# One scan through both states in twelve steps of a chunk, and wider GpSimd operands, in a bidirectional Mamba kernel

## The chip, the cores and the metric

The kernel runs on one core of a Trainium2 chip. Its time is the device time of one execution in microseconds. The engines of the core work side by side, each through its own queue in order, and wait for one another by semaphores: TensorE (PE, with its weight loads as PEld), VectorE (DVE), ScalarE (ACT), GpSimd (POOL) and SyncE (SP), which here only issues DMAs.

## The reference

The input x has 2 batches of 2048 tokens of 256 channels. A block with adaptive layer norm mixes the tokens by a Mamba layer in both directions and then runs a mixture of experts. The part that matters here is the recurrence, once forwards (weights `f_`) and once over the reversed tokens (`b_`):

```python
xz = x @ W_in.T;  xp, z = split(xz)                     # 512 inner channels
xc = silu(depthwise_conv4(xp) + b_conv)
dt, Bm, Cm = split(xc @ W_x.T, [16, 32])                # 16 states
dt = softplus(dt @ W_dt.T + b_dt);  A = -exp(A_log)
def step(h, inp):                                       # h: batch, channel, state
    dt_t, u_t, B_t, C_t = inp
    h = h * exp(dt_t[:, :, None] * A) + (dt_t * u_t)[:, :, None] * B_t[:, None, :]
    return h, einsum('bdn,bn->bd', h, C_t)
y = (ys + xc * D) * silu(z)
out = y @ W_out.T
```

So for every channel and each of 16 states there is a recurrence h[t] = decay[t] * h[t-1] + input[t] along 2048 tokens, in two batches and two directions. After it come `x + 0.5 * (forward + backward)`, a second layer norm, the gated experts (2 of 8 for a token) and a shared expert.

## The kernel before

The scan part is one hand-ordered program. Tokens are cut into chunks of 512: two directions, two batches and four chunks of tokens make 16 chunks, numbered in the order in which they are done. A chunk is 32 **steps**. Channels lie on the 128 partitions in four blocks d; states are taken two at a time (NG = 2, eight groups g). A step is one block and one group, and steps run over pairs of blocks (p), then groups, then the two blocks of the pair: an even step has the first block of a pair, the odd step after it the second, with the same two states.

What a step s does, by function:

- `inputs` (L412): GpSimd makes `db` = du times B for both states, 128x1024, three steps ahead. B is one row of numbers per state, spread over the partitions by a DMA (`load_b`), one tile for the two steps of a pair. `db` has ten buffers.
- `decays` (L429): ScalarE makes exp(dt * A), one ACTIVATE (L435) per state, 128x512, into a PSUM bank. Even and odd steps have two banks each (`banks`, L285), one tile per state.
- `scans` (L438): VectorE runs one scan (L449) per state, each from the state `hl` that the chunk before left.
- `weigh_own` (L451) or `weigh` (L457): the result times C, on VectorE per state (L455) or on GpSimd for both (L460), back into `db`. `on_pool` says which: at most odd steps it is GpSimd, at most even ones VectorE.
- `carry` (L462): ScalarE keeps the last column as the state for the next chunk (L466, L470).
- `sums` (L474): PE transposes `db` and adds all states up in PSUM (L482); this frees the `db` buffer.

After chunk 0, the four steps of two groups (one for each pair, steps 6, 7, 18 and 19) are **turned**: their operand comes from ScalarE and PE (`operands`), and the decays go into `db` in its place.

Everything else is woven into the loop over steps (L769) at written places. Three of these matter. At steps 20, 22, 24 and 26 a part of the next chunk's softplus is made: `softplus_in` (L289) takes the bank pair that the following odd step would have, ScalarE writes a sum and a logarithm into its two banks (L292, L293), and `softplus_out` (L295) works on them in three VectorE instructions (L298, L299, L300) after the scans of that step. At step 12 ScalarE runs a Silu over the next chunk's convolution (L242), with a table load on either side; at step 14 PE projects it (`dbc`, L253) and ScalarE copies the result out (L258) a step or two later. Evictions of PE's other banks by ScalarE stand behind the decays of each step.

In one turn of the loop the order is: DMAs of B and C, GpSimd's weighing of step s-2, its inputs of step s+3, the state of step s-1 (ScalarE), softplus inputs, the scans of s, softplus outputs, VectorE's weighing of s, the decays of s+1, evictions, the sums of s-4, and other units.

Of the kernel before, what the change touches and what calls it, by code (L numbers as in the profile page):

```python
# [8 lines left out]
F32 = mybir.dt.float32  # L9
AF = mybir.ActivationFunctionType  # L10
# [5 lines left out]
P = 128  # L16
# [7 lines left out]
TC = 512  # L24
# [16 lines left out]
def kernel(  # L41
# [28 lines left out]
    nc.vector.memset(eps, EPS)  # L70
    one = const.tile([P, 1], F32, tag="one", name="one")
    nc.vector.memset(one, 1.0)

    def bc(ap, n):

# [2 lines left out]
    def tiled(ap):  # L78

        return ap.rearrange("(j p) c -> p j c", p=P)  # L80

# [14 lines left out]
    with tc.tile_pool(name="mw", bufs=1) as mw, tc.tile_pool(name="mw2", bufs=2) as mw2, \  # L98
# [185 lines left out]

        def banks(s, name):  # L285

            return [ps_a.tile([P, TC], F32, tag=f"da{s % 2}_{n}", name=f"{name}_{n}") for n in range(NG)]

        def softplus_in(i, d, s):  # L289
            v = ready[i]  # L290
            v["sl"] = banks(s, f"sl{i}_{d}")
            nc.scalar.activation(v["sl"][0], v["e"][:, d, :], AF.Identity, bias=one)  # L292
            nc.scalar.activation(v["sl"][1], v["e"][:, d, :], AF.Ln, bias=one)  # L293

# [115 lines left out]
            live["C", n] = v  # L410

        def inputs(s):  # L412
            i, _, g, d = steps[s]
            db = m2.tile([P, NG, TC], F32, tag="db", bufs=NDB, name=f"db{s}")
            if not turned_step(s):
                nc.gpsimd.tensor_tensor(db, bc(ready[i]["du"][:, d, :], NG), live["B", s // 2], ALU.mult)  # L416
            live["db", s] = db

        def operands(s):

            if turned_step(s):
                i, _, _, d = steps[s]
                live["op", s] = banks(s, f"op{s}")
                for n, op in enumerate(live["op", s]):
                    for j in range(JC):
                        transpose(op[:, j * P:(j + 1) * P],
                                  ready[i]["ab"][:, n, j, d % 2 * P:(d % 2 + 1) * P], ident)

        def decays(s):  # L429
            i, _, g, d = steps[s]  # L430
            w = weights[chunks[i][0]]
            da = [live["db", s][:, n, :] for n in range(NG)] if turned_step(s) else banks(s, f"da{s}")
            for n in range(NG):
                m = g * NG + n
                nc.scalar.activation(da[n], ready[i]["dt"][:, d, :], AF.Exp, scale=w["a"][:, d, m:m + 1])  # L435
            live["da", s] = da

        def scans(s):  # L438
            i, _, g, d = steps[s]
            hl, da = state[chunks[i][:2]][0], live.pop(("da", s))  # L440
            x = live.pop(("op", s)) if turned_step(s) else [live["db", s][:, n, :] for n in range(NG)]
            h = x if turned_step(s) else da
            if on_pool(s):
                live["h", s] = m2.tile([P, NG, TC], F32, tag="h", bufs=3, name=f"h{s}")
                h = [live["h", s][:, n, :] for n in range(NG)]
            live["hs", s] = h
            for n in range(NG):
                m = g * NG + n
                nc.vector.tensor_tensor_scan(h[n], da[n], x[n], hl[:, d, m:m + 1], ALU.mult, ALU.add)  # L449

        def weigh_own(s):  # L451
            _, _, g, d = steps[s]
            if not on_pool(s):
                for n, h in enumerate(live["hs", s]):
                    nc.vector.tensor_tensor(live["db", s][:, n, :], h, live["C", s // 2][:, n, :], ALU.mult)  # L455

        def weigh(s):  # L457
            _, _, g, d = steps[s]
            if on_pool(s):
                nc.gpsimd.tensor_tensor(live["db", s], live.pop(("h", s)), live["C", s // 2], ALU.mult)  # L460

        def carry(s):  # L462
            i, _, g, d = steps[s]
# [130 lines left out]
                                     scale=v["y"][:, j, :], bias=v["mr"][:, j, :])  # L594

        def load_x(b, q):
            xt = m2.tile([P, JC, C], F32, tag="db", bufs=NDB, name=f"xt{b}_{q}")
            nc.sync.dma_start(out=xt, in_=tiled(x[b, q * TC:(q + 1) * TC, :]))
            return xt

        def norms(b, q, xt, xn):

# [13 lines left out]
            rsqrt_start(v)  # L616
            yield
            rsqrt_end(v)
            if xn is None:
                xn = m2.tile([P, JC, C], F32, tag="db", bufs=NDB, name=f"xo{u}")  # L620
            normalize(xn, v, xt)
            nc.sync.dma_start(out=tiled(xn_d[b][q]), in_=xn)

# [14 lines left out]
        make_rates(0)  # L638
        for n in range(4 * ND):
            make_conv(0, n)  # L640
        front = norms(0, 0, xts[0, 0], xns[0])
        next(front)
        next(front)
        for q in range(1, 3):
# [36 lines left out]
        def others():  # L681

            todo = [(0, 1), (0, 2), (0, 3), (1, 0), (1, 1)]
            live = []
            while todo or live:
                while todo and len(live) < 2:
                    k = todo.pop(0)
                    live.append(norms(*k, xts.pop(k), None))
                    if len(todo) > 1:
                        xts[todo[1]] = load_x(*todo[1])  # L690
                for g in list(live):
                    if next(g, 0) == 0:
                        live.remove(g)
                    yield
# [40 lines left out]
        for d in range(2):  # L735
            softplus_in(0, d, 1)
            softplus_out(0, d)
            input_(0, d)
        for s in range(3):
            inputs(s)  # L740
        decays(0)
        settle(False)
# [26 lines left out]
        for s in range(NST + 4 + SPC):  # L769
# [5 lines left out]
                weigh(s - 2)  # L775
            if s % 2 == 0 and s // 2 + 2 < NST // 2:
                load_c(s // 2 + 2)
            if s + 3 < NST:
                inputs(s + 3)
            smooth = (i + 1, soft[k]) if k in soft and i + 1 < NCH else None  # L780
            if i == 0 and k in first_soft:
# [547 lines left out]
```

## Time and profile before

| what | value |
|---|---|
| median of 3 runs | 2474.25 us (2471.53 to 2476.05) |
| the profiled execution: time, span | 2474.34 us, 2472.6 us |
| busy over the span: VectorE, GpSimd, PE, ScalarE | 2030.8, 1885.0, 1986.4, 1625.5 us |
| L416, operand on GpSimd, 128x1024 | 452 of 2361 ns |
| L449, scans, 128x512 | 1024 of about 1270 ns |
| L435, decays, 128x512 | 1024, 688 to 717 ns |
| L460, weighing on GpSimd | 252 of 2362 ns |

A group's row names the line, the engine, the operation, what it writes and reads, how often; then busy microseconds, mean nanoseconds of one, and the idle time of the engine just before such instructions, with what ended most of it. An instruction in order of time is shown by its start and its duration in microseconds, with the idle time before it and its releaser in brackets. A busy share says how full an engine is, not that it sets the pace.

### The profile page before, as it was taken

How to read it: one execution, taken by the hardware profiler on the slowest of the kernel's cores; microseconds unless marked ns; L12 is line 12 of the kernel's file. 1: busy time of each engine (PE TensorE's matmuls, PEld its weight loads, DVE VectorE, ACT ScalarE, POOL GpSimd, SP SyncE). 2: the span in 40 equal slices, each digit the busy share in tenths (PEclk: the TensorE clock that was granted, in tenths of full speed). 3: DMA queues.
4: the chain of work that ended last, by engine and by line, in shares of the span. 5: the costliest groups of instructions: out<-in, count | busy, mean ns of one | idle time of the engine just before them, and what ended most of it. 6: DMA issues, size and time to landing. Idle time of an engine off the chain costs nothing. (4 is left out here: it accounts for less than half of the span.)

```text
span 2472.6 us, 30346 instructions
## 1 busy us (share of the span) xinstructions
PE 1986.4 (80%) x9512; PEld 1372.8 (56%) x9512; DVE 2030.8 (82%) x2679; ACT 1625.5 (66%) x3377; POOL 1885.0 (76%) x991
## 2 busy tenths in 40 slices
PE   5457878788887879788887978888765487999999
PEld 2134545565555556555554656555555255788885
DVE  5499998989999999999999999999996776322333
ACT  5557787777778787777878777787753235353331
POOL 0367998989999999999999999999996405331304
PEclk9677899888998889899988989899877688999999
DMA  4344448485444454545444444444443501687863
GB/s 164 125 149 146 145 163 252 160 252 164 155 154 164 146 186 166 170 156 170 154 153 163 164 164 152 166 158 146 166 150 101 171 1 64 203 263 237 269 185 102
DMA packets 239974, 403.08 MB, mean 163 GB/s; under 512 B 38818, under 2 KB 171938, under 8 KB 239812
## 3 DMA queue, kind: packets, MB, share of 16 engines
q1 hardware_dynamic: 220724, 370.72, 46.0%
q0 software_dynamic: 6144, 16.79, 2.0%
q10 hardware_dynamic: 12944, 13.64, 1.6%
q8 instruction: 75, 1.23, 0.2%
q14 instruction: 87, 0.71, 0.1%
HBM read 346.54 MB, written 54.53 MB: 162 GB/s over the span
## 5 line engine op out<-in xcount | busy, mean ns | idle before, releaser
L416 POOL TENSOR_TENSOR db<-du,B 128x1024 f32<-128x1024 f32 x452 | 1060.0, 2361 | 13.6 <-DMA B<-bcs 13.6
L460 POOL TENSOR_TENSOR db<-h,C 128x1024 f32<-128x1024 f32 x252 | 595.1, 2362 | 66.9 <-issue 53.8
L435 ACT ACTIVATE da<-dt,w_a 128x512 f32<-128x512 f32 x904 | 594.8, 688 | 77.7 <-DVE dt L300 46.0
L482 PE MATMUL y<-ident,db 128*128 128x128 f32 x4096 | 567.7, 287 | 38.5 <-POOL db L460 36.0
L482 PEld LDWEIGHTS y<-ident,db 128*128 128x128 f32 x4096 | 504.8, 150 | 158.9 <-issue 100.8
L449 DVE TENSOR_TENSOR_SCAN da<-da,hl,db 128x512 f32<-128x512 f32 x460 | 563.9, 1273 | 4.9 <-POOL db L416 3.7
L449 DVE TENSOR_TENSOR_SCAN h<-da,hl,db 128x512 f32<-128x512 f32 x444 | 540.7, 1268 | 16.2 <-ACT da L435 16.2
L455 DVE TENSOR_TENSOR db<-da,C 128x512 f32<-128x512 f32 x460 | 293.1, 680 | 17.7 <-DMA C<-bcs 10.9
L236 PE MATMUL psc<-xp,w_conv 128*128 128x512 f32 x512 | 235.4, 603 | 10.3 <-ACT xp L225 6.4
L219 PE MATMUL psx<-xT,w_in 128*128 128x512 f32 x256 | 155.5, 727 | 100.3 <-ACT hl L470 86.9
L1041 POOL DMA_INDIRECT xs<-xs,slot x64 | 62.2, 972 | 197.3 <-DVE own L1028 95.1
L354 PE MATMUL psz<-w_in,xT 128*128 128x512 f32 x256 | 151.8, 726 | 54.0 <-ACT bT L317 32.7
L1166 POOL DMA_INDIRECT two<-ys,slot x64 | 63.0, 984 | 162.9 <-DVE hs L1068 65.5
L306 POOL TENSOR_TENSOR du<-dt,xc 128x512 f32<-128x512 f32 x64 | 81.1, 1267 | 98.3 <-DVE dt L300 97.7
L236 PEld LDWEIGHTS psc<-xp,w_conv 128*128 128x128 f32 x512 | 94.0, 193 | 108.1 <-issue 96.1
L253 PE MATMUL psd<-xc,w_x 128*48 128x512 f32 x128 | 95.8, 919 | 67.4 <-ACT hl L470 47.5
L382 PE MATMUL pso<-w_out,yg 128*128 128x256 f32 x512 | 118.4, 385 | 23.3 <-ACT e L276 23.1
L219 PEld LDWEIGHTS psx<-xT,w_in 128*128 128x128 f32 x256 | 49.8, 223 | 154.8 <-ACT hl L470 109.2
L1117 DVE COPY gT<-qgT 128x512 f32<-128x512 f32 x46 | 31.8, 692 | 121.3 <-PE qgT L846 121.1
L1062 PE MATMUL pg<-fxT,s 128*128 128x512 f32 x256 | 122.9, 638 | 0.0
L1142 ACT ACTIVATE hT<-qh,bs 128x256 f32<-128x256 f32 x92 | 38.6, 471 | 122.6 <-PE qh L1103 119.7
L382 PEld LDWEIGHTS pso<-w_out,yg 128*128 128x128 f32 x512 | 95.6, 192 | 38.5 <-ACT e L276 26.1
(200 smaller groups left out, 3221.5 us busy)
## 6 DMA issues: line engine op xcount, KB each, us to landing
C<-bcs SPq DMA_DIRECT2D x256, 512.0 KB, 4.3
B<-bcs SPq DMA_DIRECT2D x226, 512.0 KB, 4.4
we<-in_w_dram SPq DMA_DIRECT2D x138, 256.0 KB, 3.7
acc<-acc SPq DMA_DIRECT2D x32, 512.0 KB, 5.2
xs<-ident SPq DMA_DIRECT2D x2, 5888.0 KB, 23.7
xg<-xs SPq DMA_DIRECT2D x46, 256.0 KB, 3.8
ys<-yo ACTq DMA_DIRECT2D x46, 256.0 KB, 3.0
xn<-xn SPq DMA_DIRECT2D x16, 512.0 KB, 5.6
```

The lines of the kernel that those rows point to most:

```text
L219: nc.tensor.matmul(ps, w["in"][:, k, d * P:(d + 1) * P], v["xT"][:, k, :], start=(k == 0), stop=(k == KC - 1))
L236: nc.tensor.matmul(ps, w["conv"][:, d, k, :], v["xp"][:, d, k:k + TC], start=(k == 0), stop=(k == 3))
L253: nc.tensor.matmul(ps[:RK + 2 * NS, :], w["x"][:, d, :], v["xc"][:, d, :], start=(d == 0), stop=(d == ND - 1))
L354: nc.tensor.matmul(ps, v["xT"][:, k, j * P:(j + 1) * P], w["in"][:, k, DI:2 * DI], start=(k == 0), stop=(k == KC - 1))
L382: nc.tensor.matmul(ps[:, n, :], v["yg"][:, d, n * P:(n + 1) * P], wo[:, d, :], start=(d == 0), stop=(d == ND - 1))
L416: nc.gpsimd.tensor_tensor(db, bc(ready[i]["du"][:, d, :], NG), live["B", s // 2], ALU.mult)
L435: nc.scalar.activation(da[n], ready[i]["dt"][:, d, :], AF.Exp, scale=w["a"][:, d, m:m + 1])
L449: nc.vector.tensor_tensor_scan(h[n], da[n], x[n], hl[:, d, m:m + 1], ALU.mult, ALU.add)
L455: nc.vector.tensor_tensor(live["db", s][:, n, :], h, live["C", s // 2][:, n, :], ALU.mult)
L460: nc.gpsimd.tensor_tensor(live["db", s], live.pop(("h", s)), live["C", s // 2], ALU.mult)
L482: nc.tensor.matmul(ys["y"][j // 2][:, j % 2, d % 2 * P:(d % 2 + 1) * P], src[:, j * P:(j + 1) * P], ident, is_transpose=True, start=(first ...
L1062: nc.tensor.matmul(ps, s12[:, n, k, m * P:(m + 1) * P], xTs[b, q][:, k, :], start=(k == 0), stop=(k == KC - 1))
```

## The change

At an odd step that GpSimd weighs and that is not turned (twelve in each chunk), both states are scanned by one instruction of 1024 elements. So that the second state doesn't go on from the end of the first, ScalarE sets up the seam: it puts decay * state into the first input of the second state and writes zero for its first decay. The odd steps' two banks become one tile. GpSimd makes the operands of an even step and the odd step after it in one instruction, into a tile for both (five buffers of twice the size); the norms ahead of the scans use such tiles for their input and output.

```diff
         def banks(s, name):
-            return [ps_a.tile([P, TC], F32, tag=f"da{s % 2}_{n}", name=f"{name}_{n}") for n in range(NG)]
+            if s % 2:
+                v = ps_a.tile([P, NG, TC], F32, tag="da1", name=name)
+                return [v[:, n, :] for n in range(NG)], v.rearrange("p n t -> p (n t)")
+            return [ps_a.tile([P, TC], F32, tag=f"da0_{n}", name=f"{name}_{n}") for n in range(NG)], None
+
+        def through(s):
+            return s % 2 == 1 and on_pool(s) and not turned_step(s)
...
         def inputs(s):
-            db = m2.tile([P, NG, TC], F32, tag="db", bufs=NDB, name=f"db{s}")
+            db = m2.tile([P, 2, NG, TC], F32, tag="db", bufs=NDB // 2, name=f"db{s}")
             if not turned_step(s):
-                nc.gpsimd.tensor_tensor(db, bc(ready[i]["du"][:, d, :], NG), live["B", s // 2], ALU.mult)
-            live["db", s] = db
+                nc.gpsimd.tensor_tensor(
+                    db, ready[i]["du"][:, d:d + 2, :].unsqueeze(2).to_broadcast([P, 2, NG, TC]),
+                    live["B", s // 2].unsqueeze(1).to_broadcast([P, 2, NG, TC]), ALU.mult)
+            for e in range(2):
+                live["db", s + e] = db[:, e, :, :]
...
         def decays(s):
-            for n in range(NG):
+            for n in reversed(range(NG)) if through(s) else range(NG):
                 m = g * NG + n
                 nc.scalar.activation(da[n], ready[i]["dt"][:, d, :], AF.Exp, scale=w["a"][:, d, m:m + 1])
-            live["da", s] = da
+            if through(s):
+                m = g * NG + 1
+                nc.scalar.activation(db[:, 1, 0:1], da[1][:, 0:1], AF.Identity,
+                                     scale=hl[:, d, m:m + 1], bias=db[:, 1, 0:1])
+                nc.scalar.copy(da[1][:, 0:1], zero)
+            live["da", s] = da, both
...
         def scans(s):
+            if through(s):
+                nc.vector.tensor_tensor_scan(v.rearrange(flat), both, db.rearrange(flat),
+                                             hl[:, d, m:m + 1], ALU.mult, ALU.add)
+                return
...
         def load_x(b, q):
-            xt = m2.tile([P, JC, C], F32, tag="db", bufs=NDB, name=f"xt{b}_{q}")
+            xt = m2.tile([P, 2, JC, C], F32, tag="db", bufs=NDB // 2, name=f"xt{b}_{q}")
...
-        for s in range(3):
+        for s in (0, 2):
             inputs(s)
...
-            if s + 3 < NST:
+            if s % 2 == 1 and s + 3 < NST:
                 inputs(s + 3)
```

## The prediction

> **What bounds the kernel now.** I read the slices of the page first, then one steady stretch of busy times, the groups, and single instructions in order of time. The chain that ended last covers only the mixture of experts at the end, so it says nothing of the scans.
>
> ```profile
> span 2472.6 us, 30346 instructions
> ...
> DVE  5499998989999999999999999999996776322333
> ACT  5557787777778787777878777787753235353331
> POOL 0367998989999999999999999999996405331304
> ...
> L449 DVE TENSOR_TENSOR_SCAN da<-da,hl,db 128x512 f32<-128x512 f32 x460 | 563.9, 1273 | 4.9 <-POOL db L416 3.7
> L449 DVE TENSOR_TENSOR_SCAN h<-da,hl,db 128x512 f32<-128x512 f32 x444 | 540.7, 1268 | 16.2 <-ACT da L435 16.2
> ```
>
> VectorE and GpSimd are both full from slice 3 to slice 30 (about 120 to 1900 us), ScalarE is not. The stretch from 800 to 1200 us gives the shares:
>
> ```profile
> core 0: us, PE busy (x) PEld busy (x) DVE busy (x) ACT busy (x) POOL busy (x), PEclk, DMA share, GB/s
> 800.00:1200.00 400.00, 335.24 (x1690) 222.04 (x1689) 389.14 (x418) 318.15 (x671) 391.66 (x176) 0.90 0.49 164
> ```
>
> VectorE 97%, GpSimd 98%, ScalarE 80%. Which of the two full engines sets the pace is told by who waits: the scans wait 3.7 us for GpSimd's operands in the whole run, and 16.2 us for ScalarE's decays. GpSimd works three steps ahead. So VectorE sets the pace, and what moves the end is time taken from VectorE's queue or a new wait put into it.
>
> **One scan in place of two.** Twelve odd steps in each of 16 chunks, 192 in all. Start to start, the two scans of such a step take 1.190 and 1.175 us. What one element costs is read from two scans of other lengths:
>
> ```profile
> L996 DVE TENSOR_TENSOR_SCAN upto<-going,both x2: 424/424/424, 2039.4 to 2106.5; 128x128 f32<-128x128 f32 x2
> L1012 DVE TENSOR_TENSOR_SCAN end<-ones,nt x2: 174/174/174, 2044.8 to 2112.2; 128x8 f32<-128x8 f32 x2
> ```
>
> (424 - 174) / 120 = 2.083 ns an element; 512 more elements on 1.175 us make 2.242 us. A pair of 2.365 us becomes 2.242: 0.123 us saved, at most 23.7 us in 192 steps.
>
> **GpSimd's operands for two channel blocks at once.** 226 instructions of 2048 elements replace 452. L416 follows itself every 2.320 us, the 512-element L306 every 1.233 us, so an element costs 2.12 ns and an instruction saves 0.146 us: 33 us of GpSimd. GpSimd's order is otherwise the same (the odd step's operands move up next to the even step's, with nothing passed between them), so I value this at nothing: scans hardly wait for GpSimd. What hides it is the lead. An even step's operand is ready later by half the pair, some 2.2 us; the trace has medians of 3 to 9 us between its end and its scan. Only the very first scan has no lead (it waited 3.7 us for its operand): +2.2 us. Five pair buffers free one step later than ten single ones did: measured from the PE transposes that free them, 12 of 221 allocations would wait, 9 us together, on GpSimd, before step 20 whose scan has over 6 us in hand. Nothing. No DMA is added or moved; each B tile is let go by one GpSimd instruction at an earlier place in its queue.
>
> **The seam.** ScalarE gets two more instructions at each of the 192 steps, before VectorE may start: a 128x1 ACTIVATE with a pointer for the scale and one for the bias, and a 128x1 copy of zero. The nearest rows:
>
> ```profile
> L470 ACT COPY hl<-da 128x1 f32<-128x1 f32 x460 | 61.7, 157 | 83.4 <-DVE db L455 80.9
> ...
> L593 ACT ACTIVATE xt<-xt,mr_a,y_a 128x256 f32<-128x256 f32 x32 | 16.4, 589 | 10.7 <-DVE mr_a L589 10.7
> ```
>
> By size alone the seam's ACTIVATE is like the copy, 0.157 us. Against it stands the Trainium skill, "ScalarE: Activation LUTs", section "What ACT_TABLE_LOAD costs": 186 ns, 0.833 ns an element, and 93 ns more for every pointer operand, so 0.373 us. L593 has both pointers: 589 - 256 x 0.833 = 376. I take 0.376; the copy 0.157. All four operations now wait for the one before (the decays share one tile, so the second is held for the first); a dependent ScalarE instruction started 0.032 us after the other's end in this trace, and a scan 0.103 us after ScalarE. So from the release of a step's decays to its scan: 0.69 + 0.03 + 0.69 + 0.03 + 0.376 + 0.03 + 0.157 + 0.103 = 2.11 us. Before, the first scan needed only the first exponential: 0.69 + 0.10.
>
> At most steps this fits: ScalarE has a scan pair and a weighing (3.6 us) for it. In three places it does not.
>
> **Softplus steps.** At steps 20, 22, 24 and 26 of a chunk (15 chunks, 60 times) the softplus of the next chunk borrows the bank pair of the odd step that follows. L298, L299 and L300 free it:
>
> ```profile
> 1098.03 0.69 DVE L300 SCALAR_TENSOR_TENSOR dt<-dt,sl 128x512 f32<-128x512 f32 x1
> 1098.63 1.28 DVE L455 TENSOR_TENSOR db<-da,C 128x512 f32<-128x512 f32 x2
> 1098.75 0.69 ACT L435 ACTIVATE da<-dt,w_a 128x512 f32<-128x512 f32 x1 [0.77 <-DVE dt L300]
> ...
> 1099.83 2.45 DVE L449 TENSOR_TENSOR_SCAN h<-da,hl,db 128x512 f32<-128x512 f32 x2
> ```
>
> Today the first exponential is released by L298 (it started at 1097.29) and only the second waits for L300's end at 1098.72. VectorE has just L455 to do until its scan at 1099.83, 1.11 us later. With one tile for both banks, both exponentials wait for L300: 0.035 + 2.11 = 2.14 us. Stall: 2.14 - 1.11 = 1.03 us, 60 times = 61.8 us. ScalarE's next work (L470, the exponentials of the step after) slips by as much as VectorE does, so it makes no second wait. The two softplus steps early in chunk 0 lie among other idle time: nothing.
>
> **Step 17.** In 12 chunks the scan already waits, behind ScalarE's copy of the projection that PE has just made:
>
> ```profile
> 1083.10 0.58 ACT L258 COPY xd<-psd 48x512 f32<-48x512 f32 x1 [3.22 <-PE psd L253]
> 1083.58 0.19 ACT L466 COPY hl<-h 128x2 f32<-128x2 f32 x1
> 1083.67 1.30 ACT L435 ACTIVATE da<-dt,w_a 128x512 f32<-128x512 f32 x2
> 1084.47 2.46 DVE L449 TENSOR_TENSOR_SCAN h<-da,hl,db 128x512 f32<-128x512 f32 x2 [1.27 <-ACT da L435]
> ```
>
> Now it needs everything: 1083.67 + 2.11 = 1085.78, 1.31 us later; and the seam of step 11 and the ordered decays of step 13 reach L258 through L242's Silu and PE, another 0.17 + 0.09 (PE's wait takes up step 15's seam). 1.57 x 12 = 18.8 us.
>
> **Small ones.** Step 9: the second exponential ended 0.59 us before, and it comes to 0.14 late, 15 x 0.14 = 2.1 us. The two odd steps whose weighing stays on VectorE keep two scans on one tile, and the built order has the second wait for the first, and the weighing for the second. The Trainium skill, "VectorE: DVE Perf Modes", section "The DRAIN you can't avoid", says such a wait costs nothing on top of the flush; in this trace L299, which waits for L298, starts 0.03 us after its end, independent neighbours 0.09 us before. By the page 0; by the row 2 x 0.13 us at step 29 (step 13's goes into the wait of step 17), 16 times = 4.2 us. I take the row.
>
> **Sum.** Of twelve savings in a chunk, those at 5, 9, 11 and 15 run into a wait on ScalarE; eight stay: 8 x 16 x 0.123 = 15.8 us. 61.8 + 18.8 + 2.1 + 4.2 + 2.2 - 15.8 = +73.3 us. The profiled execution took 2474.34 us (span 2472.6, 1.7 around it), a tenth of a microsecond from the median of three, 2474.25 (2471.53 to 2476.05). 2474.3 + 73.3 = 2547.6 us, 3% slower.
>
> **Rivals.**
> 1. Smaller loss. VectorE's present waits inside the scans (16.2 us for decays, 14.8 for softplus inputs, 13.0 before the transposed steps) shrink when it comes later: up to 30 us back, 2517 us. With the seam at the copy's price as well (0.22 x 72 = 16), 2501. For it: such waits exist. Against: most are released by ScalarE or PE work that slips along.
> 2. Larger loss: ScalarE or PE becomes the pace. The seam adds 2 x 0.03 + 0.376 + 0.157 = 0.6 us to ScalarE at 128 steps that I count as covered, and evictions behind it feed PE. If a third reaches VectorE: 128 x 0.6 / 3 = +26 us, 2573; if a half and the full softplus term in chunk 0 too, 2588. For it: L253, L219 and L354 on PE wait for ScalarE (47.5, 86.9 and 32.7 us). Against: ScalarE waits 1 to 2 us for PE at most of those steps.
> 3. GpSimd becomes the pace because the three-level pattern with two repeated operands is slower. It has 2.5% idle (2.8 us a chunk), saves 2, and gets 4.6 from VectorE's delay: 14 pairs a chunk must each cost 0.65 us more (5.15 instead of 4.5) before it is felt. L416 already repeats one operand and keeps the rate of L306. Part of the upper end.
> 4. Faster: the long scan streams better than the short ones. VectorE must win more than it waits: 89 us over the 128 kept steps, 0.70 us each, so below 1.67 us for 1024 elements. At one nanosecond an element a scan takes 1.13 us and wins 1.23, 158 us: 2405 us. The three lengths here lie on one line (128 elements predict 512 at 1.224; 1.27 measured), so I give it little.
>
> **Chances.** The sum, 2520 to 2580: 0.72. Smaller loss (2480 to 2520): 0.12. Larger, GpSimd's included (over 2580): 0.11. Faster: 0.04; within 0.2%, about what a measurement of this kernel can tell from no change: 0.01. Slower: 0.95. The range for 8 in 10 takes in most of both neighbours: 2503 to 2590.
>
> **What would show it.** 192 scans of 1024 elements at 2.24 to 2.33 us, back to back; 226 GpSimd instructions near 4.5 us; two ScalarE rows of 192, near 0.37 and 0.16 us. Idle time before the long scan should be 80 to 100 us, released by ScalarE's copy of zero, about 1.0 us at each of steps 21, 23, 25 and 27 and 2.5 to 2.9 at step 17. VectorE's share near 1000 us should fall to 93 or 94%. Wrong if that idle row is under 40 us (the cover is longer than I read), if VectorE waits for GpSimd's operands, or if the long scan is not near 2.24 us.

## The result and the profile after

The changed kernel takes 2569.95 us (median of four runs, 2568.48 to 2573.11) beside 2475.02 us for the kernel before on the same chip: a ratio of 1.0388 (95% interval 1.037 to 1.0406), 3.9% slower. The forecast was 2547.6 us, range 2503 to 2590. The profiled execution took 2570.02 us, 95.7 more than the one of before (2474.34).

The page of the kernel after, its slices and its costliest groups (the lines have moved: L474 is the long scan, L478 the two short ones, L432 the operand, L488 the weighing on GpSimd):

```profile
span 2568.2 us, 30061 instructions
...
DVE  5499988989998989999998989999999566422333
ACT  5567787877888887877788887877775144354331
POOL 0367998989998998998988989998989503331404
...
L432 POOL TENSOR_TENSOR db<-du,B 128x2048 f32<-128x2048 f32 x226 | 1025.3, 4540 | 15.8 <-DMA B<-bcs 15.6
L488 POOL TENSOR_TENSOR db<-h,C 128x1024 f32<-128x1024 f32 x252 | 595.0, 2366 | 189.5 <-DVE h L474 187.1
...
L478 DVE TENSOR_TENSOR_SCAN da<-da,hl,db 128x512 f32<-128x512 f32 x460 | 567.6, 1274 | 10.3 <-POOL db L432 6.9
L474 DVE TENSOR_TENSOR_SCAN h<-da,hl,db 128x1024 f32<-128x1024 f32 x192 | 450.3, 2345 | 96.1 <-ACT da L459 82.5
```

The last scan now starts 1986.9 us into the span, where it started at 1891.0. VectorE is no longer full, slices of 8 and 9 take turns, and GpSimd has holes too: before its weighing it now waits 189.5 us, nearly all for scans. So GpSimd was not made the bound. The long scan takes 2.345 us for 1024 elements and VectorE stands idle before it for 96.1 us, mostly until ScalarE's copy of zero (L459). The groups of ScalarE of the kernel after, by shape, give the price of the seam:

```profile
L454 ACT ACTIVATE da<-dt,w_a 128x512 f32<-128x512 f32 x904 | 607.6, 688 | 96.4 <-DVE dt L315 87.9
L457 ACT ACTIVATE db<-da,db,hl 128x1 f32<-128x1 f32 x192 | 67.5, 352 | 17.3 <-ACT da L454 0.4
L459 ACT COPY da<-zero 128x1 f32<-128x1 f32 x192 | 31.3, 163 | 6.0
```

The ACTIVATE of one element takes 352 ns, between the 157 of the copy's row and the 376 that the prediction took from L593 and the Trainium skill. The first row's 87.9 us is the other half of the story: the exponentials now wait for the third softplus instruction (L315, before L300), where before 31.1 us of the same row (L435 there) waited for the first (L298) and 46.0 for the third (L300):

```profile
L435 ACT ACTIVATE da<-dt,w_a 128x512 f32<-128x512 f32 x904 | 594.8, 688 | 77.7 <-DVE dt L300 46.0 <-DVE e L298 31.1
```

A softplus step of the kernel after, one stretch in order of time, first VectorE's instructions and then ScalarE's (start, duration, and in brackets the idle time before it):

```profile
1260.75 2.46 DVE L478 TENSOR_TENSOR_SCAN da<-da,hl,db 128x512 f32<-128x512 f32 x2
1263.12 0.68 DVE L313 SCALAR_TENSOR_TENSOR e<-sl,e 128x512 f32<-128x512 f32 x1
1263.83 0.70 DVE L314 TENSOR_TENSOR sl<-sl,e 128x512 f32<-128x512 f32 x1
1264.57 0.69 DVE L315 SCALAR_TENSOR_TENSOR dt<-dt,sl 128x512 f32<-128x512 f32 x1
1265.17 1.28 DVE L484 TENSOR_TENSOR db<-da,C 128x512 f32<-128x512 f32 x2
1267.45 2.35 DVE L474 TENSOR_TENSOR_SCAN h<-da,hl,db 128x1024 f32<-128x1024 f32 x1 [0.99 <-ACT hl L498]
```

```profile
1265.29 1.42 ACT L454 ACTIVATE da<-dt,w_a 128x512 f32<-128x512 f32 x2 [2.90 <-DVE dt L315]
1266.80 0.35 ACT L457 ACTIVATE db<-da,db,hl 128x1 f32<-128x1 f32 x1
1267.18 0.16 ACT L459 COPY da<-zero 128x1 f32<-128x1 f32 x1
1267.28 0.21 ACT L498 COPY hl<-da 128x1 f32<-128x1 f32 x2
```

L315 ends at 1265.26 and the scan starts at 1267.45: 2.19 us, where 2.14 was predicted. VectorE has 1.28 us of weighing for it and then waits 0.99 us. (The profile names L498 as the last releaser; it started 0.17 us before the scan, and the work that the scan needs is L459's, which ended at 1267.34.)

Step by step, from the start of each scan to the start of the next one, summed over the run and compared with before: steps 20, 22, 24 and 26 lose 16.1, 16.2, 14.4 and 15.7 us, 62.4 together. The first scan comes 3.8 us later. The waits at scan 17 grow from 14.4 to 26.8 us. Those are the places that the prediction names. (VectorE's share from 800 to 1200 us is 91.5%, 366.08 of 400 us, where 93 or 94 was forecast.) It does not name step 3, which loses 11.6 us, and step 5, which loses 5.2. What lies after the last scan is unchanged.

One cut of the trace puts this in order, and the experiments below are read by it. A steady chunk (the median of chunks 3 to 13) is split at the first scans of steps 18 and 28. Before, the stretch from 18 to 28, which holds the softplus, takes 39.93 us, and the rest of the way round to the next step 18 takes 69.30, a chunk of 109.23. After, it is 43.66 and 72.38, a chunk of 116.04. So 3.73 of the 6.81 us a chunk are the softplus steps, and 3.08 are elsewhere.

### The profile page after: what moved, and what is told of

Read it like the earlier page. It is cut to its first block, busy times and chain, and to the rows that moved or that the text cites. A ratio compares the mean times of both kernels' runs of the same rounds, so it can differ in the third digit from the quotient of the medians.

```text
span 2568.2 us, 30061 instructions
## 1 busy us (share of the span) xinstructions
PE 2036.0 (79%) x9512; PEld 1401.1 (55%) x9512; DVE 2026.2 (79%) x2488; ACT 1736.5 (68%) x3761; POOL 1854.5 (72%) x765
## 5 line engine op out<-in xcount | busy, mean ns | idle before, releaser
L432 POOL TENSOR_TENSOR db<-du,B 128x2048 f32<-128x2048 f32 x226 | 1025.3, 4540 | 15.8 <-DMA B<-bcs 15.6
L488 POOL TENSOR_TENSOR db<-h,C 128x1024 f32<-128x1024 f32 x252 | 595.0, 2366 | 189.5 <-DVE h L474 187.1
L454 ACT ACTIVATE da<-dt,w_a 128x512 f32<-128x512 f32 x904 | 607.6, 688 | 96.4 <-DVE dt L315 87.9
L510 PE MATMUL y<-ident,db 128*128 128x128 f32 x4096 | 589.9, 294 | 35.5 <-POOL db L488 32.6
L510 PEld LDWEIGHTS y<-ident,db 128*128 128x128 f32 x4096 | 523.0, 154 | 160.9 <-issue 108.3
L478 DVE TENSOR_TENSOR_SCAN da<-da,hl,db 128x512 f32<-128x512 f32 x460 | 567.6, 1274 | 10.3 <-POOL db L432 6.9
L474 DVE TENSOR_TENSOR_SCAN h<-da,hl,db 128x1024 f32<-128x1024 f32 x192 | 450.3, 2345 | 96.1 <-ACT da L459 82.5
L227 PE MATMUL psx<-xT,w_in 128*128 128x512 f32 x256 | 160.0, 745 | 120.8 <-ACT xT L217 98.2
L369 PE MATMUL psz<-w_in,xT 128*128 128x512 f32 x256 | 164.3, 776 | 74.9 <-DVE acc L400 58.1
L261 PE MATMUL psd<-xc,w_x 128*48 128x512 f32 x128 | 101.5, 968 | 73.5 <-ACT ab L351 56.5
L227 PEld LDWEIGHTS psx<-xT,w_in 128*128 128x128 f32 x256 | 52.3, 234 | 176.7 <-ACT xT L217 103.2
L369 PEld LDWEIGHTS psz<-w_in,xT 128*128 128x128 f32 x256 | 59.5, 258 | 130.1 <-DVE acc L400 61.4
```

What stands on the lines that cost most here:

```text
L227: nc.tensor.matmul(ps, w["in"][:, k, d * P:(d + 1) * P], v["xT"][:, k, :], start=(k == 0), stop=(k == KC - 1))
L369: nc.tensor.matmul(ps, v["xT"][:, k, j * P:(j + 1) * P], w["in"][:, k, DI:2 * DI], start=(k == 0), stop=(k == KC - 1))
L432: nc.gpsimd.tensor_tensor(db, ready[i]["du"][:, d:d + 2, :].unsqueeze(2).to_broadcast([P, 2, NG, TC]), live["B", s // 2].unsqueeze(1).to_b ...
L474: nc.vector.tensor_tensor_scan(v.rearrange(flat), both, db.rearrange(flat), hl[:, d, m:m + 1], ALU.mult, ALU.add)
L478: nc.vector.tensor_tensor_scan(h[n], da[n], x[n], hl[:, d, m + n:m + n + 1], ALU.mult, ALU.add)
L488: nc.gpsimd.tensor_tensor(live["db", s], live["h", s], live["C", s // 2], ALU.mult)
```

## The experiments

### Which half of the change costs: e1 and e2

e1 has GpSimd's wide operands alone: two banks a step as before, two scans at every step, no seam. e2 has the scan, the seam and the shared tile, but GpSimd makes each step's operand by itself, into the changed tiles.

```diff
 e1, against the kernel after
         def banks(s, name):
-            if s % 2:
-                v = ps_a.tile([P, NG, TC], F32, tag="da1", name=name)
-                return [v[:, n, :] for n in range(NG)], v.rearrange("p n t -> p (n t)")
...
         def through(s):
-            return s % 2 == 1 and on_pool(s) and not turned_step(s)
+            return False
 e2, against the kernel after
-                nc.gpsimd.tensor_tensor(
-                    db, ready[i]["du"][:, d:d + 2, :].unsqueeze(2).to_broadcast([P, 2, NG, TC]),
-                    live["B", s // 2].unsqueeze(1).to_broadcast([P, 2, NG, TC]), ALU.mult)
+                for e in range(2):
+                    nc.gpsimd.tensor_tensor(db[:, e, :, :], bc(ready[i]["du"][:, d + e, :], NG),
+                                            live["B", s // 2], ALU.mult)
```

Expected of e1: 

> GpSimd's wide operands alone: two scans a step, the old separate banks, no seam. If VectorE sets the pace (my theory), GpSimd gets 33 us more idle time and the end stays within 5 us of the kernel before (2470 to 2480), the later first scan (+3.8 us in the changed kernel) included. If GpSimd set the pace, some 30 us are won (2445). If the wide operands are part of the loss (operands later, buffers freed later), it is slower by 10 us or more.

Expected of e2: 

> The long scan, its seam and the shared bank tile alone; GpSimd makes the operands in two instructions as before (into the same pair buffers). My theory: the whole loss is here, less the late first scan: 2563 to 2570. If the wide operands bring part of the loss: under 2555. If GpSimd's saving was needed to hold the loss down: over 2580.

Measured: e1 2477.8 us, ratio 1.0019 (1.0009 to 1.0029); e2 2573.3 us, ratio 1.0406 (1.0389 to 1.0423). The group of GpSimd's weighing before and in e1:

```profile
L460 POOL TENSOR_TENSOR db<-h,C 128x1024 f32<-128x1024 f32 x252 | 595.1, 2362 | 66.9 <-issue 53.8 <-POOL db L416 9.9 <-DVE h L449 1.6
```
```profile
L485 POOL TENSOR_TENSOR db<-h,C 128x1024 f32<-128x1024 f32 x252 | 594.7, 2365 | 101.3 <-issue 65.8
```

GpSimd's idle time before it rose from 66.9 to 101.3 us: the 33 us that the wide instructions save became idle time, and the kernel paid the later first operand (2.6 us). The whole loss is in the scan, its seam and its tile. (e2 is 3 us above the range expected of it and under the rival's 2580.)

### The softplus steps: e3, e6 and e7

e3 keeps two scans at steps 21, 23, 25 and 27, on the shared tile. e6 leaves out the seam at all steps, so that the second state goes on from the end of the first. e7 writes the zero twice.

```diff
 e3
         def through(s):
-            return s % 2 == 1 and on_pool(s) and not turned_step(s)
+            return (s % 2 == 1 and on_pool(s) and not turned_step(s)
+                    and s % SPC not in (21, 23, 25, 27))
 e6
-            if through(s):
-                m = g * NG + 1
-                nc.scalar.activation(db[:, 1, 0:1], da[1][:, 0:1], AF.Identity,
-                                     scale=hl[:, d, m:m + 1], bias=db[:, 1, 0:1])
-                nc.scalar.copy(da[1][:, 0:1], zero)
 e7
                 nc.scalar.copy(da[1][:, 0:1], zero)
+                nc.scalar.copy(da[1][:, 0:1], zero)
```

Expected of e3: 

> Steps 21, 23, 25 and 27 go back to two scans and no seam; the bank pair stays one tile. My theory: the waits of about 0.95 us at these 60 steps go, 60 savings of 0.10 us go too: 2570 - 57 + 6 = 2519 (2510 to 2530), and the idle time before the long scans falls from 96 to about 40 us. If the waits only move to the next place where ScalarE is behind: over 2545. If the shared tile alone holds the first scan up (both exponentials after the last softplus instruction), idle time stays before those two-scan steps: over 2545 as well.

Expected of e6: 

> The changed kernel without the seam's two ScalarE instructions: it leaves out the set-up of the second state's start, so the second state goes on from the first; instructions and waits are otherwise the same. My theory: about 0.6 us less at each of 60 softplus steps (36), and most of what step 31's and step 11's seams do to the chain behind steps 3, 5 and 17 (some 25): 2570 - 61 = 2509 (2498 to 2522). If the shared tile and the ordered decays are the main part: over 2535.

Expected of e7: 

> The copy of zero twice at each of 192 steps, 0.16 + 0.03 us more on ScalarE before the scan. My theory: it is felt at 60 softplus steps, and at 3, 5, 15 and 17 of 15 chunks with about one to two such lengths a chunk: 60 x 0.19 + 15 x 0.5 = 19 us, 2589 (2583 to 2597). If all twelve steps wait for the seam: 192 x 0.19 = 37 us, 2607. If ScalarE has room at the softplus steps: under 2577.

Measured: e3 2531.5 us, ratio 1.0232 (1.0211 to 1.0253). e6 2535.61, ratio 1.0082 (1.0065 to 1.0099), and e7 2621.46, ratio 1.0413 (1.0395 to 1.043). e5, e6, e7, e8 and e12 ran where the kernel before takes 2510 to 2515 us: in their traces the part behind the scans takes about 620 us in place of 582, while a steady chunk is as long as elsewhere (109.22 us in e8, 109.23 in e1). So they are compared by their ratios or by the part from the first scan to the last. Brought to 2474 us by the ratios, e6 is at 2494 and e7 at 2576. So e3 and e6 miss their ranges by 2 and 4 us, and e7 falls just into the range of the rival that ScalarE has room at the softplus steps. Its trace does not bear the rival out, as the next figures show.

The stretch from 18 to 28 is 39.93 us before, 41.42 in e3, 41.10 in e6, 43.66 after and 44.43 in e7. This splits the softplus loss. Without the seam (e6) 1.17 us of 3.73 are left, and that although four long scans save some 0.4 us in it. This is the cost of the shared tile, for one tile makes the scan wait for both exponentials. The seam makes the other 2.56, 0.64 at each of the four steps. e3 shows the tile's part without a long scan: 1.49 left, because the first of two scans waits for both exponentials too. One more copy on the path (e7) costs 0.77, 0.19 a step, as expected. In this stretch prices add up.

Outside it they do not: e7's wait at step 17 shrank by 11.1 us, although each of its long scans is released later. That was not expected.

### The rest of the chunk: e4 and e5

e4 takes two scans at step 31 alone, e5 at 17, 21, 23, 25, 27 and 31.

```diff
 e4
         def through(s):
-            return s % 2 == 1 and on_pool(s) and not turned_step(s)
+            return s % 2 == 1 and on_pool(s) and not turned_step(s) and s % SPC != 31
 e5
-            return s % 2 == 1 and on_pool(s) and not turned_step(s)
+            return (s % 2 == 1 and on_pool(s) and not turned_step(s)
+                    and s % SPC not in (17, 21, 23, 25, 27, 31))
```

Expected of e4: 

> Step 31 alone goes back to two scans and no seam. My theory for the loss at steps 3 and 5 (1.0 and 0.4 us a chunk): step 31's seam puts ScalarE's copy of the turned tokens back, PE's input projections start 0.9 us later, and the whole convolution chain up to the gating at step 4 with them. Then some 15 x 1.3 - 1.5 = 18 us come back: 2552 (2547 to 2558), and VectorE's idle time before the gating falls from 15 us to about 5. If each seam (1, 3, 5) delays PE by itself, less than 8 us come back: over 2562.

Expected of e5: 

> Two scans and no seam at steps 17, 21, 23, 25, 27 and 31; one long scan at the other six odd steps. My theory (ScalarE's seam loses time only where ScalarE or the PE chain behind it is late, and the shared bank tile keeps a remainder): what stays over the kernel before is the first scan 4 us, the two-scan steps on one tile 10 us, softplus steps 0.3 x 60 = 18 us, less six savings of 0.10 a chunk = 10 us: 2474 + 22 = 2496 (2488 to 2508). If the remaining seams at 1, 3, 5, 9, 11 and 15 cost as much as those taken away: over 2515. If they cost nothing and the remainder goes too: 2474 or less.

Measured: e4 2543.01 us, ratio 1.0282 (1.0265 to 1.0299): 27 us came back for 16 seams, where 18 us were expected. The rows of VectorE's waits for TensorE's sums at the gating, before, after, and in e4:

```profile
DVE sz L500 <- PE y L482: 4.6, 3, 3.6
```
```profile
DVE sz L528 <- PE y L510: 15.4, 15, 3.4
```
```profile
DVE sz L528 <- PE y L510: 4.0, 2, 3.4
```

That is step 3's loss: 15 waits after, 2 or 3 in the others. In the trace of the kernel after, counted from scan 28, ScalarE's second copy of the normalized tokens (L217) comes 0.92 us later. In e4 it still comes 0.28 us later, so the seam of step 31 makes 0.64. The half of TensorE's projection that reads it (L227) starts 0.93 us later, and VectorE waits 0.98 us for the sums that stand behind the projection in TensorE's queue. The clock has a part in it. The first eight matmuls of the projection end 1.63 us later than before in the kernel after, but 0.51 earlier than before in e4, although they begin their second half 0.28 us late: the mean granted clock over them is 0.65 before, 0.59 after and 0.73 in e4.

e5 missed by far. Its ratio is 1.0196 (1.0176 to 1.0216), which is 2523 us where the kernel before takes 2474, and 2488 to 2508 were expected. The part with the scans takes 1831.7 us in it, 1840.6 in e3, 1786.7 before: taking away the causes of e3 and e4 together gave 9 us more than e3 alone, where e4 alone had given 27. Two gains, each real by itself, did not add.

### A gain for VectorE, and one for ScalarE, ahead of step 17: e8 and e11

Both are the kernel before with a relief. e8 is e1 with step 28 weighed by GpSimd. e11 lets VectorE keep the last columns of steps 10, 12 and 14.

```diff
 e8, against e1
         def on_pool(s):
-            return s % SPC in (4, 16) or d % 2 == 1 and g != NGR - 2
+            return s % SPC in (4, 16, 28) or d % 2 == 1 and g != NGR - 2
 e11, against the kernel before
                     m = g * NG + n
-                    nc.scalar.copy(hl[:, d, m:m + 1], hs[n][:, TC - 1:TC])
+                    if s % SPC in (10, 12, 14, 16):
+                        nc.vector.tensor_copy(hl[:, d, m:m + 1], hs[n][:, TC - 1:TC])
+                    else:
+                        nc.scalar.copy(hl[:, d, m:m + 1], hs[n][:, TC - 1:TC])
```

Expected of e8: 

> GpSimd's wide operands alone (as in the run that had them alone, 2478 us), and step 28 weighed on GpSimd too: two 0.68 us instructions of VectorE (1.19 us start to start) a chunk go, one of 2.36 us on GpSimd comes in 16 chunks. My theory that VectorE sets the pace, and that GpSimd waits for scans about 4 us a chunk with the wide operands: 16 x 1.19 = 19 us off, 2459 (2455 to 2466), faster than the kernel before. If GpSimd is as full as VectorE: 2475 or more.

Expected of e11: 

> The kernel before, but the last columns of steps 10, 12 and 14 (two 128x1 copies each, 0.157 us on ScalarE) are kept by VectorE. If the ScalarE and PE chain sets the pace ahead of step 17, taking 0.94 us a chunk from it and giving VectorE some 0.4 us makes the kernel faster: what lies behind the Silu of step 12 counts, 0.3 to 0.9 us x 13 chunks = 4 to 12 us less, and VectorE's wait at step 17 shrinks by it plus VectorE's own 0.4 us. If VectorE sets the pace there too: 0.4 x 16 = 6 us more.

(Step 16 in e11's list is weighed by GpSimd and takes the other branch, so three steps change.) Measured: e8 1.0021 (1.0011 to 1.003), nothing gained: the 17.8 us that VectorE saved at step 28 came back as 14.9 us of waiting at scan 30, for decays that stand behind ScalarE's Silu of step 28. So the time is that of the rival (2475 or more), but the engine that was full there is ScalarE and not GpSimd: in the kernel before, the first exponential of step 30 ends only 0.15 us before its scan starts. e11 0.9997 (0.9985 to 1.0008), no difference, which neither of its two expectations had: VectorE's copies cost 0.13 us at each of the three steps, its wait at step 17 fell from 14.4 to 8.7 us, and the chunk took 109.22 us. Time taken from VectorE at step 28, or moved from ScalarE to VectorE ahead of step 17, did not change the length of this part. Other places were not tried.

### A delay for ScalarE alone, at two places: e9 and e10

```diff
 e9, against the kernel before (e10: 23 in place of 31)
             for n in range(NG):
                 m = g * NG + n
                 nc.scalar.activation(da[n], ready[i]["dt"][:, d, :], AF.Exp, scale=w["a"][:, d, m:m + 1])
+            if s % SPC == 31:
+                m = g * NG
+                nc.scalar.activation(spare, one, AF.Identity, scale=hl[:, d, m:m + 1], bias=one)
+                nc.scalar.copy(spare, one)
+                nc.scalar.copy(spare, one)
```

Expected of e9: 

> The kernel before with nothing of the change in it; after the decays of step 31 ScalarE gets three small instructions more (a 128x1 ACTIVATE with two pointers and two 128x1 copies, into a tile that nobody reads), some 0.75 us with their waits, once in each chunk. Theory that from step 28 to step 17 a chain of ScalarE and PE sets the pace and that step 31's seam reaches it through ScalarE's copy of the normalized tokens for PE: all of it comes out in the time, 0.75 x 15 = 11 us, seen as a longer wait of VectorE between steps 3 and 17 (+8 to +13 us on the part with the scans). Rival that VectorE sets the pace all through: no scan of step 31 or 0 waits for these instructions, so at most 2 us.

Expected of e10: 

> The same three instructions, but after the decays of step 23, inside the stretch of steps 18 to 28. Theory that VectorE alone sets the pace there: ScalarE has to wait for VectorE's softplus anyway and the extra work is hidden, 0 to +3 us on the part with the scans. Rival that ScalarE's work costs wherever it is put: as much as at step 31, 8 to 13 us.

Measured: e9 2482.15 us, ratio 1.0034 (1.0022 to 1.0045); e10 2475.23, ratio 1.0009 (1.0 to 1.0019), which is as expected for e10. In e9 step 3 loses 1.02 us and step 5 0.35 in a steady chunk, with no long scan anywhere: so step 31's seam, and not the long scan, is what step 3 pays for. But of 11 us expected on the part with the scans 6.0 were lost. The loss at steps 3 and 5, 1.37 us, was won back between steps 11 and 18 (20.98 us in place of 22.35), where the wait at scan 17 went from 1.27 us to nothing, and the steady chunk took 109.23 us, as before. Why scan 17 came earlier is told by TensorE's projection ahead of it (L253; L254 in e9). Three stretches, each from the first of its eight matmuls to the end of the last, of before and of e9 (length, TensorE busy, weight loads, granted clock, DMA share, GB/s):

```profile
1076.62:1083.06 6.44, 6.44 (x8) 1.45 (x8) 0.56 0.24 80
1185.80:1192.26 6.46, 6.46 (x8) 1.45 (x8) 0.56 0.20 76
1295.03:1301.49 6.46, 6.46 (x8) 1.45 (x8) 0.56 0.19 75
```
```profile
1084.63:1089.70 5.07, 5.07 (x8) 1.21 (x8) 0.71 0.06 20
1193.82:1198.91 5.09, 5.09 (x8) 1.21 (x8) 0.71 0.05 19
1303.03:1308.13 5.10, 5.10 (x8) 1.21 (x8) 0.71 0.04 16
```

The same eight matmuls take 6.45 us at a granted clock of 0.56 and 5.08 at 0.71: 1.37 us, just what had been lost earlier. In a chunk near the start of the kernel before they took 3.6 us. The clock changes in steps: in every trace here it is 1.0 or 0.5, and it changes only at marks 3.41 us apart that run on through the whole kernel. The kernel before around the first of these stretches, cut at the marks (busy us of TensorE, weight loads, VectorE, ScalarE, GpSimd, then the clock):

```profile
1068.66:1072.07 3.41, 3.02 (x27) 2.74 (x26) 3.41 (x5) 3.38 (x3) 3.41 (x2) 1.00 0.73 244
1072.07:1075.48 3.41, 0.90 (x9) 0.66 (x7) 3.41 (x5) 3.38 (x8) 3.41 (x3) 1.00 0.21 64
1075.48:1078.90 3.42, 2.28 (x3) 0.64 (x4) 3.42 (x5) 3.42 (x11) 3.42 (x3) 0.50 0.50 153
1078.90:1082.31 3.41, 3.41 (x5) 0.81 (x4) 3.41 (x4) 0.98 (x2) 2.56 (x2) 0.50 0.02 5
1082.31:1085.72 3.41, 3.41 (x23) 2.46 (x22) 2.14 (x3) 2.62 (x7) 3.41 (x3) 1.00 0.22 61
```

In the second row TensorE is busy for only 0.90 of 3.41 us. It waits 3.65 us for ScalarE, and from the next mark on it runs at half clock. What ScalarE has to do first is not the Silu of step 12 itself, which ended 4.35 us before L253 starts. It is L336, four instructions that read `psu` out of one of the two PSUM banks that `psd` takes turns with. They stand behind the Silu in ScalarE's queue, and in each of chunks 2 to 15 L253 starts 0.05 us after the last of them. (The profile names L470, which runs just behind L336. In one of these chunks L470 comes later, and the 0.05 us is the same.) No run moved L336.

The third row is filled to two thirds and the clock stays low; the fourth is full and the clock comes back. Over chunks 3 to 13 of the kernel before, the clock fell after 43 windows of 3.41 us, in which TensorE was busy for at most 61%, and came back after 43, all at least 83% busy (a full clock was kept through windows down to 45%, so between 45 and 61% it went either way). This is what the Trainium skill describes in "TensorE: Matmul & The Clock Gate", section "What's actually happening": a window of 3413 ns that runs on by itself, half clock after an idle one, full clock after a busy one. The traces agree on the window and on the two clocks. The section does not say how idle or how busy a window has to be: here 0.90 us of work in one did not keep the clock.

The busy share is not all of the rule. In these chunks of the kernel before the clock also stayed at half after 25 windows, two of them over 80% busy. In the kernel after it did so in ten of these eleven chunks at step 19 or 20, after a window in which TensorE was busy for at least 96% with the sums (L510) and the small projection `pst` (L276). Why those windows did not bring the clock back is open.

### Less work for TensorE: e12

e12 is the changed kernel with half of the sums on TensorE left out.

```diff
 e12, against the kernel after
             db = live.pop(("db", s))
-            for n in range(NG):
+            for n in range(1, NG):
                 add(db[:, n, :], False, g == NGR - 1 and n == NG - 1)
```

Expected: 

> The changed kernel, but TensorE adds up only the second of the two states of each step (eight 128x128 transposes less at every pair of steps; the first state is left out of y, nothing else is). VectorE, GpSimd and ScalarE keep every instruction. In the traces so far TensorE's granted clock falls to half in windows of 3.41 us, 6.0 of them in a steady chunk before and 9.2 after, and a chunk lasts 32.0 of these 3.41 us before and 34.0 after. Theory that this clock is what holds the stretch from step 28 to step 18: with less for TensorE to do the windows get fewer (under 6 a chunk), the stretch from 18 to 28 keeps its 43.7 us, the rest loses its waits on TensorE at steps 3, 5 and 17, 72.4 becomes 68 to 69.5, and a chunk takes 111.6 to 113.2 us and needs not be a whole number of 3.41: 2505 to 2535 us where the kernel before takes 2474. Rival that the order of ScalarE's instructions (the seam of step 31 ahead of its copies for TensorE) holds it: 115 to 116 us a chunk and 2555 to 2570 us.

Measured: ratio 1.0228 (1.0211 to 1.0245), which is 2531 us where the kernel before takes 2474. The stretch from 18 to 28 kept its 43.66 us and the rest fell from 72.38 to 68.88, below the 69.30 of before; a chunk took 112.54 us. The time is what the theory of TensorE said, and the rival's 2555 to 2570 is out. But the windows of half clock did not get fewer: some 12 a chunk. A steady chunk of before, after, and of e12, from step 18 to step 18 (length, busy us of TensorE, weight loads, VectorE, ScalarE, GpSimd, then the clock):

```profile
1305.56:1414.78 109.22, 91.21 (x463) 60.59 (x461) 106.45 (x116) 85.72 (x179) 107.14 (x49) 0.91 0.46 159
1414.78:1524.01 109.23, 91.18 (x463) 60.57 (x461) 106.37 (x115) 85.61 (x179) 107.09 (x49) 0.91 0.46 160
```
```profile
1485.73:1601.78 116.05, 94.96 (x462) 62.72 (x461) 106.18 (x104) 92.51 (x203) 105.25 (x35) 0.87 0.44 150
1601.78:1717.82 116.04, 94.96 (x462) 62.72 (x461) 106.17 (x103) 92.52 (x203) 105.29 (x35) 0.87 0.43 150
```
```profile
1343.44:1455.98 112.54, 83.74 (x333) 49.76 (x332) 105.86 (x105) 92.95 (x203) 105.20 (x35) 0.82 0.47 155
1455.98:1568.53 112.55, 82.94 (x333) 49.01 (x332) 105.78 (x104) 92.94 (x203) 105.17 (x35) 0.82 0.45 155
```

With fewer instructions TensorE has more idle windows, so it is slowed more often (0.82 against 0.87), and its 333 instructions still take 83 us. That part of the expectation had the sign of the rule wrong, so the time came out as forecast, but not by the way that was forecast. What e12 shows is that TensorE's queue is in the path from step 28 to step 18, since nothing else was made shorter. How much of the gain would have come with a full clock it cannot show.

### All of them by the chunk

Medians over chunks 3 to 13; the number of windows is that on which the chunks settle, the last column a mean. "Rest" is the chunk less the stretch from 18 to 28.

| kernel | step 18 to 28, us | rest, us | chunk, us | in windows of 3.413 us | windows at half clock |
|---|---|---|---|---|---|
| before | 39.93 | 69.30 | 109.23 | 32.00 | 6.0 |
| e1 wide operands | 39.92 | 69.31 | 109.23 | 32.00 | 5.7 |
| e8 step 28 weighed by GpSimd | 39.92 | 69.30 | 109.22 | 32.00 | 5.9 |
| e9 delay at 31 | 39.92 | 69.31 | 109.23 | 32.00 | 4.3 |
| e10 delay at 23 | 39.92 | 69.30 | 109.22 | 32.00 | 6.0 |
| e11 copies on VectorE | 39.92 | 69.30 | 109.22 | 32.00 | 6.0 |
| e6 no seam | 41.10 | 69.46 | 110.56 | 31.6 to 32.8 | 6.1 |
| e12 half the sums | 43.66 | 68.88 | 112.54 | 32.97 | 11.7 |
| e5 two scans at six steps | 41.42 | 71.21 | 112.63 | 33.00 | 6.7 |
| e3 two scans at softplus | 41.42 | 71.22 | 112.64 | 33.00 | 7.2 |
| e4 two scans at 31 | 43.65 | 69.12 | 112.77 | 33.0 | 7.5 |
| after | 43.66 | 72.38 | 116.04 | 34.00 | 9.2 |
| e2 the scan alone | 43.86 | 72.19 | 116.05 | 34.00 | 9.2 |
| e7 zero twice | 44.43 | 71.82 | 116.25 | 34.0 | 8.7 |

Most of these kernels settle on chunks of whole windows, 32, 33 or 34. (e4 has single chunks of 33.8; e7 begins at 34.0 to 34.9; e6 goes round between 31.65, 32.4 and 32.35 and doesn't settle; e12 stays a little under 33.) The place of scan 17 within its window shows how: in chunks 6 to 11 of the kernel before it is 2.57, 2.24, 2.16, 2.13, 2.13 and 2.13 us after a mark. It runs into a fixed place, and each deviation is about a quarter of the one before. Why a deviation should shrink can be argued from the psd matmuls: those that start 1 us late while the end of the half clock is fixed have 1 us less of half clock to run in, half a microsecond of work at full clock, and so end only half a microsecond late.

## Why the prediction was right

Its sign, its range and its main term are right, its centre is 22 us low. By its own steps:

- **One scan for two.** 2.345 us where 2.242 to 2.33 was named; a step with it is 0.10 us shorter from start to start, not 0.123. Of eight savings kept, worth 15.8 us, those that lie between steps 18 and 28 moved the end. Those outside probably did not: e8 shows it for a gain at step 28, no run for steps 1, 3, 17 and 31.
- **Wide operands at nothing.** Right: 1.0019 by themselves, of which the first scan is 2.6 us. In the whole change the first scan came 3.8 us later (2.2 predicted).
- **Softplus steps.** 62.4 us (61.8 predicted), by the named way: 2.19 us from release to scan (2.14). e6 and e3 show both causes, the seam with two thirds and the shared tile with one.
- **The seam's price.** The ACTIVATE took 352 ns. The rule of the pointers was nearer (376) than the row of the copy (157).
- **Step 17 and step 9.** The wait at step 17 alone grew by 12.4 us. The predicted 18.8 us is how much later scan 17 starts, and counted from scan 11 that is 18.2 us in the run, for steps 13 and 14 had lost 4.9 and 4.3 us on the way. So the size is right. The way from the exponentials to the scan is as described; what reaches `psd` ahead of it comes through L336 and its PSUM bank, not straight from the Silu. Step 9 lost 2.4 us (2.1). ScalarE at a step 17 of the kernel after, in order of time (the scan started at 1251.42, 2.08 us after the exponentials did; 2.11 predicted, with 0.06 too little ahead of the seam and 0.07 too much behind the copy):

```profile
1248.76 0.58 ACT L266 COPY xd<-psd 48x512 f32<-48x512 f32 x1 [2.53 <-PE psd L261]
1249.24 0.19 ACT L494 COPY hl<-h 128x2 f32<-128x2 f32 x1
1249.34 1.42 ACT L454 ACTIVATE da<-dt,w_a 128x512 f32<-128x512 f32 x2
1250.85 0.35 ACT L457 ACTIVATE db<-da,db,hl 128x1 f32<-128x1 f32 x1
1251.23 0.16 ACT L459 COPY da<-zero 128x1 f32<-128x1 f32 x1
```

- **Two scans on one tile.** Steps 13 and 29 lose 0.30 us each (0.26 predicted), 9.7 us in the run. From the first scan to the second it is 1.32 us there (1.19 before), and from the second to the weighing 1.33 (1.18). The rule that such a wait costs nothing on top ("VectorE: DVE Perf Modes", "The DRAIN you can't avoid") is not what this kernel shows at these steps, where a scan writes into the tile that it reads. Where the two scans write into another tile (steps 21 to 27 in e3) they are still 1.20 us apart.
- **The step that failed** is "VectorE sets the pace", taken for the whole chunk, and with it the sum of stalls and the reason given against rival 2, that ScalarE has time to spare. It holds between steps 18 and 28, where the prices add up and e10's delay is hidden. From 28 to the next 18 TensorE's queue is in the path; its waits for ScalarE cost it its clock; and chunks last whole windows. In this rest the prediction has, per chunk, 1.57 + 0.14 + 0.26 less four savings of 0.123, 1.5 us. It was 3.08. The difference, 1.6 us in 15 chunks, is 24 us, about all of the error of 22. The largest part of it is at steps 3 and 5 (16.8 us), which the prediction put at nothing. They pay for the seam of step 31, which e4 takes away and e9 makes without the change; e6, without any seam, has a rest of 69.46 us. Rival 2 had named this way, a seam that reaches VectorE through ScalarE's evictions and TensorE, and with 2573 us came nearer than the sum.

What is shown and what is not: that most kernels settle on whole windows, that the clock falls after windows in which TensorE had little to do, that psd's time changes with it, that the seam of step 31 costs what steps 3 and 5 lose, and that TensorE's queue is in the path of the rest are measured. That the window is the cause of the whole numbers is inferred, from the grid's length and from the way the place in it settles; no run had the clock held. Read so, the table suggests why e5 missed. VectorE has 1.37 us of slack before scan 17 in a chunk of 32 windows (from start to start), just what e9 used up. The softplus stalls (3.73 us) are more than that and make it 33, as e4 shows; with step 31's seam it is 34. e3 brings the stalls down to 1.49 us, still more than the slack: 33 windows, and e5, which takes away step 31's seam as well, has the same 1.49 us and so the same 33. e6 does not fit in: its 1.17 us are less than the slack, but its chunks take 31.6 to 32.8 windows. No variant was faster than the kernel before; e11 equals it.

## What to carry to other kernels

Where one instruction takes the place of two, count from the release to its start: with one tile for both halves the first half waits for the last writer, and two ScalarE instructions of one element each made that 0.6 us longer, much more than the 0.1 us that the longer scan saved. Before you add up stalls over a loop, ask in each stretch which engine's queue carries the delay on, and look at the granted clock window by window around every wait of TensorE: in this loop of 109 us, losses of up to 1.4 us in a chunk changed nothing, and others came out as whole windows of 3.41 us. Two fixes of such a loop are tested together, since their gains need not add.

## What the hardware showed that was not expected

- Less work for TensorE gave it a lower clock: 333 instructions a chunk at 0.82, where 462 had 0.87 (e12). The eight psd matmuls took from 3.6 to 6.6 us with the clock they met.
- A loop of 109 us settled on a grid of 3.41 us by its ninth chunk and kept 32.00 windows under five different edits, among them three more instructions for ScalarE (e9) and 1.2 us less for VectorE a chunk (e8).
- Where e5 to e8 and e12 ran, the part behind the scans takes 620 to 625 us in place of 582, with a mean granted clock there of 0.89 to 0.90 against 0.92 to 0.93; a steady chunk is as long as elsewhere. The cause is open.
